# Layer 0 of a hybrid attention network: projections in two column tiles, column biases for both heads at once, and the first unit ahead of the branch

## The chip, the cores and the metric

The kernel runs on one core of a Trainium2 chip. The metric is the device time of one execution in microseconds (us). All arithmetic is in float32. A core has these engines: PE (TensorE: weight loads and matrix products), DVE (VectorE), ACT (ScalarE), POOL (GpSimd), and SP, which here only starts transfers. Each engine works through its own queue in order and waits for the others with semaphores.

## The reference, cut to what matters

The network has four layers on an image of 2 x 64 x 64 pixels with 128 channels. The change touches layer 0 alone, an attention with relative position biases, 4 heads of 32 dimensions and 4096 pixels for each of the 2 images:

```python
qkv = jnp.einsum('bhwc,cd->bhwd', x, w_qkv)          # x is the group-normalised input
...
pos = relative_position_bias(pos_q, pos_emb_h, pos_emb_w).reshape(B, nh, L, L)
scores = jnp.einsum('bnqd,bnkd->bnqk', q, k) * scale + pos
attn = jax.nn.softmax(scores, axis=-1)
out = jnp.einsum('bnqk,bnkd->bnqd', attn, v)
```

The bias of a query pixel (x, y) and a key pixel (x', y') is a row part, q times a row embedding that depends on x' - x, plus a column part, q times a column embedding that depends on y' - y. The result is added to the input. Three more layers follow: a triangle product, an attention without softmax with a mixture of experts behind it, and a softmax attention with a second mixture.

## The kernel before, in words

`layer0` first transposes the input to channels by pixels (`xT`) and normalises it, image by image. For each image it also takes the largest squared length of a pixel's vector (`l0sq`, the products `l0n`, the maximum `l0most`). From these and the weights it bounds the scores. The program then branches (L384): if the bound is small enough, which it is for this input, `l0_bounded` runs, where softmax needs no maximum; otherwise `l0_any` runs.

`l0_bounded` works through 8 units: image b, pair of heads, and half of the queries (2048 of them). A unit has 4 query groups of 512 (`qb`), and each group goes over 32 blocks of 128 keys. One block is:

- 4 products on PE for the scores of two heads, `l0sc` (L590). The operand `ka` holds for each head 32 rows of keys and 32 rows that are a one-hot code of the key's row; the operand `qa` holds 32 rows of queries and 32 rows of row bias. So the row part of the bias comes out of the same product.
- on ACT the exponential of the 128 x 1024 scores into `l0es` (L598).
- on DVE the product of this with `ew`, the exponential of the column part of the bias (L601).
- 4 products on PE with the values, `l0o` (L549), issued two blocks later.

Two buffers hold scores, three hold `l0es`, and two PSUM buffers, called `misc`, serve everything else. What the next unit needs is made meanwhile by a generator, `l0_prepare`. After every second block the loop takes one piece of it, up to its next yield (`piece`). A second list of odd work (`extra`: statistics for layer 1, and the head of layer 1 for the first image) is taken up after every fourth block. The listed order is then rearranged by the framework's scheduler, engine by engine; data dependencies stay.

`l0_prepare` of a unit consists of
- `l0pq`: 4 products that project the queries, with weights `wqk`, a copy of the weights spread so that the two heads of a pair land on rows 0 to 31 and 64 to 95. Each result is copied by ACT and by DVE into the two planes of `qa`.
- `l0pw`: the column bias, 64 columns y times 2 heads, each a product with a weight window of its own from the embedding table `pe` and 32 columns of queries; 8 exponentials on ACT write `ew`; two transfers copy the results to the other 64 partitions.
- `l0ph`: the row bias, 64 products, 16 copies into `qa`.
- for the first half of a pair, `l0pk`: 8 products that project the keys, 16 copies into `ka`.

The first unit has nothing to be hidden behind, and its whole `l0_prepare` runs after the branch. The values of an image (`l0_values`, 32 products, 8 copies) are made before its first `l0o`.

Of the kernel before, what the change touches and what calls it, by code (L numbers as in the profile page):

```python
# [14 lines left out]
P = 128  # L15
# [24 lines left out]
class Net:  # L40
# [216 lines left out]
    def layer0(self, xT, gst, na, nb):  # L257
# [3 lines left out]
        with ExitStack() as st:  # L261
# [3 lines left out]

            pe = wp.tile([P, 2, 2 * S - 1], F32, tag="pe", name="l0pe")
            with (
# [5 lines left out]
                for i, n in enumerate("hw"):  # L273
                    nc.scalar.dma_start(
                        out=raw[: 2 * S - 1, i, :], in_=ins[f"L0_conv_pos_emb_{n}"]
                    )
                    pt = ps.tile([P, 512], F32, tag="misc", name=f"l0pe{n}")
                    nc.tensor.transpose(pt[:HD, :P], raw[:, i, :], self.ident)
                    for lo in (0, 64):
                        nc.scalar.copy(pe[lo : lo + HD, i, :], pt[:HD, : 2 * S - 1])  # L280
# [68 lines left out]
                most = ap.tile([P, 4], F32, tag="most", name="l0most")  # L349
                for b in range(B):  # L350
# [3 lines left out]
                    for half in range(2):  # L354
                        part = xT[:, b, half * 2048 : (half + 1) * 2048]
                        nc.vector.tensor_scalar(part, part, gm, gr, ALU.subtract, ALU.mult)
                        sq = ap.tile([P, 2048], F32, tag="sq", name=f"l0sq{b}_{half}")
                        if half:
                            nc.gpsimd.tensor_tensor(sq, part, part, ALU.mult)
                        else:  # L360
                            nc.scalar.activation(sq, part, AF.Square)
                        pn = ps.tile([P, 512], F32, tag="misc", name=f"l0n{b}_{half}")
                        for i in range(4):
                            nc.tensor.matmul(
                                pn[HD * i : HD * (i + 1), :],
                                lhsT=ones,
                                rhs=sq[:, i * 512 : (i + 1) * 512],
                                start=True,
                                stop=True,
                            )  # L370
                        nc.vector.tensor_reduce(
                            most[:, 2 * b + half : 2 * b + half + 1], pn, AX.X, ALU.max
                        )
# [10 lines left out]
                small = self.at_most("l0", s1, 60.0)  # L384
            with tc.If(small > 0) as fits:
                self.l0_bounded(xT, w, pe, gst, na, nb)
            with fits.Else():
                self.l0_any(xT, w, pe)
# [78 lines left out]
    def l0_bounded(self, xT, w, pe, gst, na, nb):  # L467
# [15 lines left out]
        with (  # L483
# [4 lines left out]

            wqk = wp.tile([P, 2, 2, 2, 64], F32, tag="wqk", name="wqk")
            nc.vector.memset(wqk, 0.0)  # L490
            nc.vector.tensor_copy(
                wqk[:, :, :, :, :HD].rearrange("p j a h d -> p (j a h) d"),
                w[:, : 2 * C].rearrange("p (g d) -> p g d", d=HD),
            )
            kas = []
            for i in range(2):
                ka = wp.tile([P, L], F32, tag=f"ka{i}", name=f"ka{i}")
                for lo in (32, 96):
                    for half in range(2):
                        nc.gpsimd.tensor_copy(  # L500
                            ka[lo : lo + 32, half * H2 : (half + 1) * H2].rearrange(
                                "p (x y) -> p x y", y=S
                            ),
                            self.ident[lo : lo + 32, lo : lo + 32]
                            .unsqueeze(2)
                            .broadcast_to([32, 32, S]),
                        )
                kas.append(ka)
            v1 = wp.tile([P, NC, NH, HD + 1], F32, tag="v1", name="l0v1")
            nc.vector.memset(v1[:, :, :, HD:], 1.0)  # L510
# [8 lines left out]
            made = {}  # L519
            side, extra = [], []  # L520

# [15 lines left out]
            side.append(self.l0_prepare(ap, ps, units[0], xT, wqk, pe, kas, made))  # L537
            ready(units[0])
            waiting = []

            def values():
                unit, qb, k, es = waiting.pop(0)
                b, pair, half = unit
                if k == 0 and (pair, half, qb) == (0, 0, 0):
# [11 lines left out]
                if k == NC - 1:  # L556
# [5 lines left out]
                    if (b, pair, half, qb) == (0, 1, 1, 3):  # L562

                        extra.append(
                            self.l1_first(ps, xT[:, 0, :], gst[:, 0], w[:, : 2 * C], na, nb)
                        )
# [7 lines left out]
            for i, unit in enumerate(units):  # L574
# [4 lines left out]
                if i + 1 < len(units):  # L579
                    side.append(self.l0_prepare(ap, ps, units[i + 1], xT, wqk, pe, kas, made))  # L580
# [33 lines left out]
    def l0_prepare(self, ap, ps, unit, xT, wqk, pe, kas, made):  # L614
# [7 lines left out]
        qa = ap.tile([P, 2, H2], F32, tag="qa", name=f"l0qa{t}")  # L622
        ew = ap.tile([P, 2, H2], F32, tag="ew", name=f"l0ew{t}")
        for g in range(H2 // 512):
            cols = slice(g * 512, (g + 1) * 512)
            pq = ps.tile([P, 512], F32, tag="misc", name=f"l0pq{t}_{g}")
            nc.tensor.matmul(
                pq,
                lhsT=wqk[:, 0, pair, :, :].rearrange("p h d -> p (h d)"),
                rhs=xT[:, b, half * H2 + g * 512 : half * H2 + (g + 1) * 512],  # L630
                start=True,
                stop=True,
            )
            nc.scalar.copy(qa[:, 0, cols], pq)
            nc.vector.tensor_copy(qa[:, 1, cols], pq)
            yield
        for g in range(4):

            pw = ps.tile([P, 16, S // 2], F32, tag="misc", name=f"l0pw{t}_{g}")
            for i in range(16):  # L640
                y = 16 * g + i
                for lo in (0, 64):
                    nc.tensor.matmul(  # L643
                        pw[lo : lo + 64, i, :],
                        lhsT=pe[lo : lo + HD, 1, S - 1 - y : 2 * S - 1 - y],
                        rhs=qa[lo : lo + HD, 0, y::S],
# [3 lines left out]
                if i % 8 == 7:  # L650
                    yield
            for h in range(2):
                rows = slice(64 * h, 64 * h + 64)
                dst = ew[rows, h, :].rearrange("p (x y) -> p y x", y=S)
                nc.scalar.activation(dst[:, 16 * g : 16 * g + 16, :], pw[rows], AF.Exp)

        nc.sync.dma_start(out=ew[64:128, 0, :], in_=ew[0:64, 0, :])
        nc.sync.dma_start(out=ew[0:64, 1, :], in_=ew[64:128, 1, :])
# [22 lines left out]
        if half == 0:  # L681
            ka = kas[pair]
            root = float(HD) ** -0.5
            for g in range(L // 512):
                cols = slice(g * 512, (g + 1) * 512)
                pk = ps.tile([P, 512], F32, tag="misc", name=f"l0pk{b}_{pair}_{g}")
                nc.tensor.matmul(
                    pk,
                    lhsT=wqk[:, 1, pair, :, :].rearrange("p h d -> p (h d)"),
                    rhs=xT[:, b, cols],  # L690
                    start=True,
                    stop=True,
                )
# [1560 lines left out]
```

## Time and profile before

| what | value |
|---|---|
| time, median of 3 runs | 4827.95 us (4826.84 to 4828.98) |
| profiled execution, its own time | 4826.12 us |
| its span, first to last instruction | 4824.3 us |
| PE busy | 4514.4 us |
| DVE busy | 2918.7 us |
| ACT busy | 2661.0 us |
| POOL busy | 945.1 us |
| branch taken | about 58.2 us |
| first `l0o` of the first unit | 115.48 us |
| last `l0o` of layer 0 | about 2130 us |

Busy time is the time in which an engine has an instruction under way. Every float32 product appears in the profile as two records; a transpose appears as one. A number such as 64*33 after the names of a matmul is the part of the array that it uses, contraction rows by output rows. "[0.73 <-ACT l0os L558]" means that the engine stood idle for 0.73 us before the instruction and that the named instruction ended this. Layer 0 fills the first 2131 us of the span.

### The profile page before, as it was taken

What the parts mean: (1) busy time and instruction counts of PE and PEld (TensorE: products, weight loads), DVE (VectorE), ACT (ScalarE), POOL (GpSimd) and SP (SyncE); (2) the same over time, 40 slices, a digit from 0 to 9 for tenths busy, and PEclk for the clock granted to TensorE, in tenths of its full rate; (3) what the DMA queues carried; (4) which work ended last, traced back from release to release, by engine and by line L of the source; (5) the groups of instructions that cost most, each with busy time, mean ns of one, the idle gap of its engine ahead of it and who ended that gap; (6) DMA issues with size and microseconds to landing.
All of it is one profiled execution on the core that took longest, in us unless ns stands there. A gap on an engine that the chain in (4) does not pass through costs nothing.

```text
span 4824.3 us, 78221 instructions
## 1 busy us (share of the span) xinstructions
PE 4514.4 (94%) x33260; PEld 1761.8 (37%) x33260; DVE 2918.7 (61%) x4784; ACT 2661.0 (55%) x3091; POOL 945.1 (20%) x848
## 2 busy tenths in 40 slices
PE   6999999999999999978799999999977999999999
PEld 3333333333233333325322223322225444444443
DVE  4676767676766767766746666555553444454447
ACT  4666565655656565555667666676731444433326
POOL 1000000000000000004455454555531000000008
PEclk7999999999999999989899999999987999999999
DMA  1000000000000000000000000000025000000001
GB/s 46 10 1 10 1 10 1 10 1 10 1 1 10 1 12 1 1 6 21 6 1 1 1 1 1 1 1 1 1 93 194 1 1 0 1 0 1 0 1 36
DMA packets 43211, 60.30 MB, mean 12 GB/s; under 512 B 4352, under 2 KB 25056, under 8 KB 41696
## 3 DMA queue, kind: packets, MB, share of 16 engines
q1 hardware_dynamic: 41552, 54.34, 3.6%
q8 instruction: 265, 4.34, 0.4%
q10 hardware_dynamic: 1296, 0.82, 0.1%
q14 instruction: 98, 0.80, 0.1%
HBM read 42.56 MB, written 4.19 MB: 10 GB/s over the span
## 4 chain that ended last, share of the span: by engine, by line
PE 78%; DVE 9%; ACT 6%; POOL 3%; issue 2%; DMA 1%; SPq 0%; DVEq 0%; ACTq 0%; POOLq 0%
PE l0sc L590 17%; PE l0o L549 16%; PE scl L2076 9%; PE oTl L2035 9%; PE l2sc L1448 5%; PE l2pos L1195 5%; PE l2av L1494 3%; DVE l2es L1468 2%; PE f3ex L2185 2%; POOL l2es L1471 2%; PE l0pw L643 1%; ACT l2es L1479 1%; ACT l0es L598 1%; PE l1p L938 1%; ACT l2es L1459 1%
## 5 line engine op out<-in xcount | busy, mean ns | idle before, releaser
L601 DVE TENSOR_TENSOR l0es<-l0es,l0ew 128x1024 f32<-128x1024 f32 x1024 | 1253.4, 1228 | 586.4 <-ACT l0es L598 586.1
L598 ACT ACTIVATE l0es<-l0sc 128x1024 f32<-128x1024 f32 x1024 | 1042.8, 1024 | 676.2 <-PE l0sc L590 671.0
L549 PE MATMUL l0o<-l0es,l0v 64*33 64x512 f32 x8192 | 1068.0, 591 | 19.8 <-ACT l0os L558 12.5
L590 PE MATMUL l0sc<-l0qa,ka 64*64 64x512 f32 x8192 | 1080.6, 596 | 4.7 <-ACT l0es L598 4.7
L1479 ACT ACTIVATE l2es<-l2es 128x1024 f32<-128x1024 f32 (+3 forms) x576 | 559.5, 984 | 265.8 <-POOL l2es L1471 258.7
L1471 POOL TENSOR_TENSOR l2es<-l2es 128x1024 f32<-128x1024 f32 (+3 forms) x352 | 581.2, 1662 | 493.9 <-DVE l2es L1468 442.7
L2043 DVE TENSOR_TENSOR accl<-accl,esl 128x1024 f32<-128x1024 f32 x240 | 302.5, 1261 | 424.6 <-ACT esl L2087 421.2
L1468 DVE TENSOR_SCALAR l2es<-l2sc 128x1024 f32<-128x1024 f32 (+3 forms) x320 | 338.7, 1058 | 314.5 <-PE l2sc L1448 314.3
L2087 ACT ACTIVATE esl<-scl 128x1024 f32<-128x1024 f32 x240 | 245.6, 1023 | 485.2 <-PE scl L2076 460.1
L590 PEld LDWEIGHTS l0sc<-l0qa,ka 64*64 64x64 f32 x8192 | 294.3, 133 | 545.6 <-issue 478.4
L2076 PE MATMUL scl<-l3qT,l3kT 128*128 128x512 f32 x1024 | 487.4, 596 | 0.0
L549 PEld LDWEIGHTS l0o<-l0es,l0v 64*33 64x33 f32 x8192 | 257.2, 108 | 626.8 <-issue 559.2
L1448 PE MATMUL l2sc<-l2q,kept 32*128 32x512 f32 (+3 forms) x2304 | 391.3, 622 | 83.4 <-ACT l2es L1459 58.9
L2035 PE MATMUL oTl<-esl,l3v 128*128 128x512 f32 x960 | 451.1, 592 | 0.0
L724 POOL TENSOR_TENSOR x<-x,l0y 128x256 f32<-128x256 f32 x32 | 23.4, 731 | 2037.1 <-DVE l0y L719 1912.6
L1494 PE MATMUL l2av<-l2es,kept 128*32 128x512 f32 (+3 forms) x2304 | 312.2, 592 | 0.0
L1195 PE MATMUL l2pos<-kept 128*32 128x512 f32 x2416 | 296.8, 599 | 0.1
L2035 PEld LDWEIGHTS oTl<-esl,l3v 128*128 128x128 f32 x960 | 181.7, 190 | 225.6 <-issue 222.0
L2076 PEld LDWEIGHTS scl<-l3qT,l3kT 128*128 128x128 f32 x1024 | 188.2, 191 | 207.5 <-issue 191.3
L1459 ACT ACTIVATE l2es<-l2sc 128x1024 f32<-128x1024 f32 x224 | 226.1, 1010 | 53.2 <-PE l2sc L1448 51.8
L1448 PEld LDWEIGHTS l2sc<-l2q,kept 32*128 32x128 f32 x2304 | 116.1, 187 | 328.3 <-ACT l2es L1459 160.2
L1195 PEld LDWEIGHTS l2pos<-kept 128*32 128x32 f32 x2416 | 78.4, 111 | 175.1 <-issue 174.3
(702 smaller groups left out, 3750.0 us busy)
## 6 DMA issues: line engine op xcount, KB each, us to landing
f2w<-in_L_ffn_weight_dram SPq DMA_DIRECT2D x32, 1024.0 KB, 13.1
l0ew<-l0ew SPq DMA_DIRECT2D x16, 512.0 KB, 5.0
x<-in_x_dram SPq DMA_DIRECT2D x8, 512.0 KB, 8.9
out_dram<-x SPq DMA_DIRECT2D x16, 256.0 KB, 2.3
kept<-in_L_attn_pos_rev_dram SPq DMA_DIRECT2D x1, 1792.0 KB, 6.7
ew<-in_L_ffn_expert_w_dram SPq DMA_DIRECT2D x1, 512.0 KB, 4.0
kept<-in_L_attn_pos_rev_dram SPq DMA_DIRECT2D x1, 256.0 KB
f2b<-in_L_ffn_weight_dram ACTq DMA_DIRECT2D x2, 128.0 KB, 2.7
```

What stands on the lines that cost most here:

```text
L549: nc.tensor.matmul(o[64 * h : 64 * h + HD + 1, r, :], lhsT=v1[rows, k, 2 * pair + h, :], rhs=es[rows, h, :], start=(k == 0), stop=(k == NC ...
L590: nc.tensor.matmul(sc[64 * c : 64 * c + 64, h, :], lhsT=ka[rows, k0 : k0 + 64], rhs=qa[rows, k // (NC // 2), qs], start=True, stop=True,)
L598: nc.scalar.activation(es, sc, AF.Exp)
L601: nc.vector.tensor_tensor(es, es, ew[:, :, qs], ALU.mult)
L1195: nc.tensor.matmul(out[part], lhsT=lhsT[:, part], rhs=rhs, start=start, stop=stop)
L1448: nc.tensor.matmul(sc[:, h2, off:], lhsT=kT[hs, k * P : (k + 1) * P], rhs=q[hs, off:], start=True, stop=True,)
L1468: nc.vector.tensor_scalar(es[:, :, lo:], sc[:, :, lo:], root, None, ALU.mult)
L1471: nc.gpsimd.tensor_tensor(part, part, part, ALU.mult)
L1479: nc.scalar.activation(es[:, :, off:], es[:, :, off:], AF.Silu)
L1494: nc.tensor.matmul(avs[i][hs, off:], lhsT=v[:, k, hs], rhs=es[h // 2][:, h % 2, off:], start=(k == 0), stop=last,)
L2035: nc.tensor.matmul(oT, lhsT=vs[b][:, k, :], rhs=es[:, i, :], start=(k == 0), stop=(k == NC - 1),)
L2076: nc.tensor.matmul(sc[:, i, :], lhsT=kTs[b][:, k * P : (k + 1) * P], rhs=qT[:, qb * 512 : (qb + 1) * 512], start=True, stop=True,)
```

## The change

In words:

- **Projections.** `wqk` is gone. A new helper, `projected`, issues two products of 64 output rows each (both heads of the pair, straight from `w`) for two neighbouring groups of 512 pixels, into the two halves of one PSUM tile. `l0pq` is thus called 2 times for a unit and not 4, `l0pk` 4 times for a pair and not 8.
- **Copies of the queries.** For every 512 queries there are now six copies out of PSUM, three on ACT (64 x 512, 32 x 256, 32 x 1024) and three on DVE (32 x 512, 32 x 256, 32 x 256), where there was one 128 x 512 on each. They place the queries of both heads side by side on rows 32 to 63 (columns y below 32) and 96 to 127 (the others). These rows hold the row bias later.
- **Column bias.** One product of a weight window now takes 64 columns, the queries of both heads: 64 products for a unit and not 128. The two row groups write two PSUM tiles at once, 8 of them to a piece. The exponentials stay 8 of 64 x 512. One transfer of 1024 KB replaces two of 512 KB.
- **First unit.** Its `l0_prepare`, its one-hot rows and the values of the first image are issued ahead of the branch, mixed with the maxima. For this the two images are transposed and normalised first, and the maxima follow. `qa` and `ew` are now tiles outside the branch (`qe`, and `qe1` for every second unit).
- `l1_first` gets a tile of its own (`gb`) for what it wrote over the projection weights before, since `w` is still read. `l0_any` is adapted and isn't run for this input.

```diff
+            qe = wp.tile([P, 2, 2, L // 2], F32, tag="qe", name="l0qe")
+            ka = wp.tile([P, L], F32, tag="ka", name="ka0")
+            self.l0_hot(ka, 0)
+            self.l0_hot(ka, 1)
+            v = wp.tile([P, NC, NH, HD + 1], F32, tag="v1", name="l0v1")
...
-                    for lo in (0, 64):
-                        nc.scalar.copy(pe[lo : lo + HD, i, :], pt[:HD, : 2 * S - 1])
+                    for lo in range(0, P, 32):
+                        copy = nc.vector.tensor_copy if lo % 64 else nc.scalar.copy
+                        copy(pe[lo : lo + HD, i, :], pt[:HD, : 2 * S - 1])
...
+                first = self.l0_prepare(
+                    ps, (0, 0, 0), xT, w, pe, [ka], (qe[:, 0], qe[:, 1]), made
+                )
...
+                for b in range(B):
+                    for half in range(2):
+                        pieces(4)
+                        lengths(b, half)
...
                 small = self.at_most("l0", s1, 60.0)
+                for _ in first:
+                    pass
+                self.l0_values(ps, 0, xT, w, v)
             with tc.If(small > 0) as fits:
-                self.l0_bounded(xT, w, pe, gst, na, nb)
+                self.l0_bounded(xT, w, pe, gst, na, nb, qe, ka, v)
...
+        def projected(j, g, name):
+
+            out = ps.tile([P, 512], F32, tag="misc", name=name)
+            for i in range(2):
+                nc.tensor.matmul(
+                    out[64 * i : 64 * i + 64, :],
+                    lhsT=w[:, j * C + 64 * pair : j * C + 64 * pair + 64],
+                    rhs=xT[:, b, (g + i) * 512 : (g + i + 1) * 512],
+                    start=True,
+                    stop=True,
+                )
+            return out
+
+        for g in range(0, H2 // 512, 2):
+            pq = projected(0, half * (H2 // 512) + g, f"l0pq{t}_{g}")
+            for i in range(2):
+                cols = slice((g + i) * 512, (g + i + 1) * 512)
+                p0 = pq[64 * i : 64 * i + 32]
+                p1 = pq[64 * i + 32 : 64 * i + 64]
+                left = [
+                    v.rearrange("p (x y) -> p x y", y=S)[:, :, : S // 2]
+                    for v in (qa[32:64, 0, cols], p0)
+                ]
+                yield
+                nc.scalar.copy(qa[:64, 1, cols], pq[64 * i : 64 * i + 64])
+                nc.vector.tensor_copy(qa[:HD, 0, cols], p0)
+                yield
+                nc.vector.tensor_copy(left[0], left[1])
+                for h, p in ((0, p0), (1, p1)):
+                    right = [
+                        v.rearrange("p (x y) -> p x y", y=S)[:, :, S // 2 :]
+                        for v in (qa[96:128, h, cols], p)
+                    ]
+                    (nc.scalar.copy if h else nc.vector.tensor_copy)(right[0], right[1])
+                nc.scalar.copy(
+                    qa[64 : 64 + HD, :, cols], p1.unsqueeze(1).broadcast_to([HD, 2, 512])
+                )
             yield
         for g in range(4):
-            pw = ps.tile([P, 16, S // 2], F32, tag="misc", name=f"l0pw{t}_{g}")
-            for i in range(16):
-                y = 16 * g + i
-                for lo in (0, 64):
+            pw = [
+                ps.tile([P, 8, 2, S // 2], F32, tag="misc", name=f"l0pw{t}_{g}_{i}")
+                for i in range(2)
+            ]
+            for n in range(8):
+                for i, lo in ((0, 32), (1, 96)):
+                    y = 32 * i + 8 * g + n
                     nc.tensor.matmul(
-                        pw[lo : lo + 64, i, :],
+                        pw[i][:S, n, :, :],
                         lhsT=pe[lo : lo + HD, 1, S - 1 - y : 2 * S - 1 - y],
-                        rhs=qa[lo : lo + HD, 0, y::S],
+                        rhs=qa[lo : lo + HD, :, y::S],
                         start=True,
                         stop=True,
                     )
...
-        nc.sync.dma_start(out=ew[64:128, 0, :], in_=ew[0:64, 0, :])
-        nc.sync.dma_start(out=ew[0:64, 1, :], in_=ew[64:128, 1, :])
+        nc.sync.dma_start(out=ew[S:], in_=ew[:S])
...
-            for g in range(L // 512):
-                cols = slice(g * 512, (g + 1) * 512)
-                pk = ps.tile([P, 512], F32, tag="misc", name=f"l0pk{b}_{pair}_{g}")
+            for g in range(0, L // 512, 2):
+                pk = projected(1, g, f"l0pk{b}_{pair}_{g}")
                 yield
-                nc.scalar.activation(ka[:HD, cols], pk[:HD], AF.Copy, scale=root)
-                nc.vector.tensor_scalar(
-                    ka[64 : 64 + HD, cols], pk[64 : 64 + HD], root, None, ALU.mult
-                )
+                for i in range(2):
+                    cols = slice((g + i) * 512, (g + i + 1) * 512)
+                    lo = 64 * i
+                    nc.scalar.activation(ka[:HD, cols], pk[lo : lo + HD], AF.Copy, scale=root)
+                    nc.vector.tensor_scalar(
+                        ka[64 : 64 + HD, cols], pk[lo + HD : lo + 64], root, None, ALU.mult
+                    )
```

In the order in which the engines of the changed kernel get their instructions, the copies of a pair of query groups stand close together. Around blocks 7 to 11 of a unit's first query group ACT's queue is: exponential 7, copy 64 x 512, exponential 8, copies 32 x 256, 32 x 1024 and 64 x 512, exponential 9, copies 32 x 256 and 32 x 1024, exponential 10. DVE's queue is: product 7, copies 32 x 512, 32 x 256, 32 x 256, product 8, the same three copies, product 9. The second of ACT's copies waits for DVE's third, the first of DVE's waits for ACT's first, and so on along one PSUM tile.

## The prediction

> **What bounds the kernel now.** I read the page first, for the bound and the chain that ended last.
>
> ```profile
> span 4824.3 us, 78221 instructions
> ...
> PE 4514.4 (94%) x33260; PEld 1761.8 (37%) x33260; DVE 2918.7 (61%) x4784; ACT 2661.0 (55%) x3091; POOL 945.1 (20%) x848
> ...
> PE 78%; DVE 9%; ACT 6%; POOL 3%; issue 2%; DMA 1%; SPq 0%; DVEq 0%; ACTq 0%; POOLq 0%
> PE l0sc L590 17%; PE l0o L549 16%; PE scl L2076 9%; PE oTl L2035 9%; PE l2sc L1448 5%; PE l2pos L1195 5%; PE l2av L1494 3%; DVE l2es L1468 2%; PE f3ex L2185 2%; POOL l2es L1471 2%; PE l0pw L643 1%; ACT l2es L1479 1%; ACT l0es L598 1%; PE l1p L938 1%; ACT l2es L1459 1%
> ```
>
> PE sets the time, and layer 0's loop is a third of the chain. Next, busy time by stretches (width, then PE, PEld, DVE, ACT, POOL, granted clock):
>
> ```profile
> 58.00:102.00 44.00, 34.88 (x412) 22.61 (x414) 15.17 (x23) 19.55 (x27) 14.96 (x8) 0.64 0.11 25
> 102.00:340.00 238.00, 236.35 (x2370) 86.87 (x2370) 159.19 (x144) 145.43 (x154) 2.19 (x3) 1.00 0.03 6
> 1181.27:1197.15 15.88, 13.95 (x92) 5.54 (x88) 8.04 (x18) 6.90 (x8) 0.00 (x0) 0.68 0.00 1
> ```
>
> In the loop PE is full (236 of 238 us); ACT and DVE are not (145, 159). So whatever leaves PE's queue there shortens the layer. The start, 58 to 102, is no PE bound: the first unit is made alone, at a clock of 0.64. Third, PE in order of time, where a piece's price can be read:
>
> ```profile
> 121.87 1.04 PE L549 MATMUL l0o<-l0es,l0v 64*33 64x512 f32 x8
> 122.84 1.12 PE L627 MATMUL l0pq<-xT,wqk 128*128 128x512 f32 x2
> ...
> 126.52 1.04 PE L549 MATMUL l0o<-l0es,l0v 64*33 64x512 f32 x8
> ...
> 131.17 1.04 PE L549 MATMUL l0o<-l0es,l0v 64*33 64x512 f32 x8
> 132.14 1.13 PE L643 MATMUL l0pw<-l0qa,l0pe 32*64 32x32 f32 x32
> ...
> 168.37 1.04 PE L549 MATMUL l0o<-l0es,l0v 64*33 64x512 f32 x8
> 169.34 1.15 PE L666 MATMUL l0ph<-l0qa,l0pe 32*64 32x64 f32 x32
> ...
> 173.04 1.04 PE L549 MATMUL l0o<-l0es,l0v 64*33 64x512 f32 x8
> ```
>
> Two blocks without a piece take 3.44 us (`l0o` at 207.93 and 211.37). With a `l0pq` piece they take 126.52 - 121.87 = 4.65, with `l0pw` (131.17 to 135.82) 4.65, with `l0ph` 4.67. A piece costs 1.21, 1.21 and 1.24 us; `l0pk` (454.50 to 459.15) 1.21.
>
> **Pieces removed, units 2 to 8.** `l0pq`: 4 to 2 pieces, 7 x 2 x 1.21 = 16.9 us. `l0pk`: 8 to 4, in 3 units, 3 x 4 x 1.21 = 14.5. `l0pw`: 8 pieces of 16 products to 4 of 16 with twice the columns, 7 x (8 x 1.21 - 4 x 1.24) = 33.0. Together **64.4 us**.
>
> Two prices aren't in the trace. Two 128 x 64 products side by side cost 1.21 if they overlap, 2.07 if not (one more 0.86, `l0pq`'s pace). I take 1.21: the four 128*32 tiles of `l0n` ran as 8 records in 1.94 us at a cold clock, where 8 x 0.43 = 3.44 at full clock would be one after another. The new `l0pw` piece is 32 records of 64 columns, two row groups over the same array columns. Near row: `l0ph`, same size, 1.24. Low end 1.21; high end 2.06 if nothing overlaps (32 x 0.43 x 64/512 = 1.71, and 0.35 for switching, which is what a `l0pq` piece costs above its 2 x 0.43). I take 1.24, since `l0sc` overlaps row groups over the same columns.
>
> **What ACT and DVE pay.** Before, 512 queries cost ACT 0.585 and DVE 0.69. Now ACT has 64 x 512 (0.58), 32 x 256 (between 0.29 and 0.575; 0.36 by the line through 32 x 512 at 0.575 and 97 x 1024 at 1.009) and 32 x 1024 (1.01); DVE has 0.69 and two of 32 x 256 (0.35 to 0.69; 0.42, as L719 with 128 x 256). By busy time that is hidden: per unit 4 x 1.4 us more on ACT, in 250 us with 90 idle. But it comes in a burst, and the two engines take turns on one PSUM tile, as today:
>
> ```profile
> 170.59 0.57 ACT L677 COPY l0qa<-l0ph 32x512 f32<-32x512 f32 x1 [0.62 <-PE l0ph L666]
> 171.48 0.68 DVE L677 COPY l0qa<-l0ph 32x512 f32<-32x512 f32 x1
> 172.20 0.58 ACT L677 COPY l0qa<-l0ph 32x512 f32<-32x512 f32 x1 [1.03 <-DVE l0qa L677]
> 172.80 1.94 ACT L598 ACTIVATE l0es<-l0sc 128x1024 f32<-128x1024 f32 x2
> 172.81 0.70 DVE L677 COPY l0qa<-l0ph 32x512 f32<-32x512 f32 x1 [0.64 <-ACT l0qa L677]
> ```
>
> ACT stands 1.03 us for DVE, with the next exponential queued behind it. PE doesn't notice, because every second block brings another piece, 1.24 us of cover. In the changed order the copies of one `l0pq` tile fall into four blocks without a piece. I follow the three queues, with `l0sc` 8 starting at 0, an `l0sc` or `l0o` each 0.86, an exponential 1.02 and a product with `ew` 1.23:
> - ACT: copy to 0.74, exponential 8 to 2.22, wait for DVE's third copy (to 2.37), three copies 2.41 to 4.43, exponential 9 to 5.48, wait for DVE's sixth (to 6.05), two copies to 7.49, exponential 10 to 8.54.
> - DVE: three copies 0.78 to 2.37, product 8 to 3.63, wait for ACT's fourth copy, three copies 4.47 to 6.05, product 9 to 7.31, product 10 to 9.81.
> - PE, with two score buffers and `l0o` two blocks behind: `l0sc` 11 is due at 5.21 and waits for exponential 9 (0.34); `l0o` 9 for product 9 (0.96); `l0sc` 12 for exponential 10 (0.37); `l0o` 10 for product 10 (0.41). After that the queues catch up.
>
> That is 2.1 us a tile; 14 tiles in units 2 to 8: **29.4 us given back**.
>
> A pair of `l0pw` exponentials holds ACT for 2.14 us. The exponential behind it ends 3.33 us after its `l0sc` began, its product with `ew` at 4.6, and `l0o` is due at 4.30. Today the next piece covers that; the new `l0pw` pieces stand four blocks apart. 28 x 0.35 = **9.8 us**. The key copies keep a piece every second block, as `l0ph` today: nothing.
>
> [...] The idle shares alone would give 0 for this step, 39 us less; [...]
>
> **The first unit.** Before, the branch is at 58.15 and the first `l0o` at 115.48, with `l0sc` 0 to 2, one `l0pq` and the values done. After, in the order of the changed queues:
> - Both images' statistics come first. Image 0's ends at 27.7. DVE then has 8 statistics of image 1 (0.61 each), image 0's chain and its two scalings (2.6), to 36.7; image 1's chain 3.45 and scalings, to 42.8. PE's first `l0pq` stands behind image 1's chain, at about 39.
> - Two tiles of turns, 7.2 us each for six copies on either engine, and four maxima on DVE (0.69), to about 55.
> - On ACT a table load (1.28) and six exponentials (1.05), to 63; the bound's root with two more loads, to 66; two exponentials, 68.5.
> - `l0ph`'s 8 copies on ACT with their waits 5.5, keys 5, values 8 x 0.59: 84.5. ACT is the longest queue; PE and DVE wait for it.
> - Branch 0.9 (58.1 to 59.0 today), `l0sc` 0 at 85.4, `l0o` 0 four us later (product and exponential between), at 89.5.
>
> Gain **26 us**; 18 to 34, as the turns overlap less or more.
>
> Beside it: POOL's one-hot copies (4 x 1.9 us) move to the start, where POOL is idle until 31.8; `ka1`'s follow the branch, two units before use. Behind SP's transfer stands only its branch load. 1024 KB: 10 us as two of 5.0, 13.1 as the weights' row; issued at 68.5, wanted at 87. Later units have some 90 blocks. If it came late, product 0 would wait for it. The memsets of `l0o` and `l0os` (2 x 0.91 on DVE) run during the first scores. The four copies into `pe` on DVE (about 0.26, ACT's row at 9.29) fit in DVE's idle 1.42 us before 16.58.
>
> **Sum.** 4826.1 (the profiled execution) - 26 - 64.4 + 39.2 = 4774.9. The median of the runs is 1.8 above the profiled one: **4776 us**.
>
> **Rivals.**
> - *The bursts cost nothing*: 4776 - 39 = 4737. For: today's bursts cost nothing. Against: the cover is gone.
> - *Tiles don't overlap*: the `l0pw` piece at 2.06 gives 28 x 0.82 = 23 back, 4799; the column pairs at 2.07, 26 x 0.86 = 22, 4798. The second would be a change that doesn't do what it says. `l0n` and `l0sc` speak against both.
> - *The start gains nothing*: ACT's serial queue ends as late as today's, 4802. With the tiles too: about 4825, no change.
> - *Slower: each burst drops the clock.* It happens today, once:
>
> ```profile
> 1184.59 0.35 PE L135 MATMUL gpv<-gv,gmat 128*128 128x1 f32 x2 [1.93 <-DVE gv L133]
> ...
> 1188.55 1.91 PE L643 MATMUL l0pw<-l0qa,l0pe 32*64 32x32 f32 x30
> ```
>
> After that wait a piece took 1.91, and the stretch (clock 0.68) 15.9 us where 3 blocks (5.2), a piece (1.2) and the statistics' products (1.5) make 7.9: 8 lost. At 8 x 14 = 112: 4888. It decides from 3.7 us a burst. [...] and `l0o` at 189.99 resumed at full pace after 0.73. I go by these.
>
> **How the numbers follow.** Forecast 0.48; bursts free 0.17; tiles 0.18; start 0.09; start and tiles 0.03; clock 0.05. Range: 4734 takes in the free bursts, 4804 the tiles and the start; outside lie the clock and double cases. 0.2% (9.7 us) is about what the measurement tells from no change. Faster 0.92, same 0.03, slower 0.05.
>
> **What would show it.** `l0pq`, `l0pk` and `l0pw` pieces at 1.2 us between `l0o`; PE waits of 0.3 to 1 us for `l0es` on ACT and DVE after each `l0pq`; first `l0o` near 90. Wrong if a `l0pw` piece takes 2 us, PE never waits after `l0pq`, the clock falls below 1 in the loop, or the first `l0o` is past 105.

## The result, and the profile after

The changed kernel takes 4785.74 us (median of 4 runs, 4780.16 to 4790.27), against 4827.76 for the kernel before on the same chip: a ratio of 0.9912 (95% interval 0.9895 to 0.9929), 42 us or 0.9% faster. The forecast was 4776. The sum holds a large error that a smaller one of the other sign half hides, so the agreement says less than it seems to. The profiled execution took 4783.74, its span is 4781.9, so 42.4 us less than before. The page of the changed kernel:

```profile
span 4781.9 us, 76270 instructions
...
PE 4464.8 (93%) x32236; PEld 1739.6 (36%) x32236; DVE 2943.9 (62%) x4850; ACT 2697.7 (56%) x3157; POOL 945.6 (20%) x848
...
PE 75%; DVE 11%; ACT 7%; issue 3%; POOL 2%; DMA 1%; SPq 0%; DVEq 0%; ACTq 0%; POOLq 0%
```

PE is still the bound, with 50 us less work. The chain that ended last now runs over DVE for 11% and ACT for 7%, where it was 9 and 6, and PE spends some of what it no longer does waiting. PE in order of time (start, duration, engine, line, operation, what is written and read, part of the array, shape, count, and idle time before with what ended it), first the start of the loop and one `l0pq` piece:

```profile
87.41 1.95 PE L615 MATMUL l0sc<-l0qe,ka 64*64 64x512 f32 x16
...
91.68 1.06 PE L573 MATMUL l0o<-l0es,l0v 64*33 64x512 f32 x8 [0.29 <-DVE l0es L626]
...
596.83 1.04 PE L573 MATMUL l0o<-l0es,l0v 64*33 64x512 f32 x8
597.80 1.08 PE L657 MATMUL l0pq<-xT,wqkv 128*64 128x512 f32 x4
...
599.72 1.04 PE L573 MATMUL l0o<-l0es,l0v 64*33 64x512 f32 x8
...
603.15 1.04 PE L573 MATMUL l0o<-l0es,l0v 64*33 64x512 f32 x8
604.24 1.09 PE L615 MATMUL l0sc<-l0qe,ka 64*64 64x512 f32 x8
606.08 1.06 PE L573 MATMUL l0o<-l0es,l0v 64*33 64x512 f32 x8 [0.74 <-DVE l0es L626]
607.30 1.09 PE L615 MATMUL l0sc<-l0qe,ka 64*64 64x512 f32 x8 [0.16 <-ACT l0es L623]
608.55 1.06 PE L573 MATMUL l0o<-l0es,l0v 64*33 64x512 f32 x8 [0.17 <-DVE l0es L626]
...
610.30 1.04 PE L573 MATMUL l0o<-l0es,l0v 64*33 64x512 f32 x8
```

The first `l0o` comes at 91.68 (115.48 before). The `l0pq` piece with its two column tiles costs 599.72 - 596.83 - 1.72 = 1.17 us, no more than the single product before, so the tiles overlap. Then come four late starts: `l0sc` at 604.24, `l0o` at 606.08, `l0sc` at 607.30 and `l0o` at 608.55 are 0.23, 0.98, 0.36 and 0.39 us later than the pace of 0.86 allows. From 596.83 to 610.30 it takes 13.47 us, where six blocks (10.30) and the piece make 11.47: the tile costs PE 2.0 us more. Of the 13 `l0pq` tiles in the loop, 11 cost between 1.95 and 2.03 us in this way; behind the other two another product follows at once. ScalarE's queue in the same time:

```profile
601.14 0.36 ACT L686 COPY l0qe<-l0pq 32x256 f32<-32x256 f32 x1 [0.15 <-DVE l0qe L686]
601.53 1.00 ACT L687 COPY l0qe<-l0pq 32x1024 f32<-32x1024 f32 x1
602.56 0.58 ACT L677 COPY l0qe<-l0pq 64x512 f32<-64x512 f32 x1
603.17 1.02 ACT L623 ACTIVATE l0es<-l0sc 128x1024 f32<-128x1024 f32 x1
604.80 0.37 ACT L686 COPY l0qe<-l0pq 32x256 f32<-32x256 f32 x1 [0.61 <-DVE l0qe L686]
605.19 1.01 ACT L687 COPY l0qe<-l0pq 32x1024 f32<-32x1024 f32 x1
606.22 1.94 ACT L623 ACTIVATE l0es<-l0sc 128x1024 f32<-128x1024 f32 x2
```

Three copies stand ahead of one exponential and two ahead of the next. The `l0pw` piece of the changed kernel:

```profile
637.50 1.04 PE L573 MATMUL l0o<-l0es,l0v 64*33 64x512 f32 x8
638.47 1.98 PE L701 MATMUL l0pw<-l0qe,l0pe 32*64 32x64 f32 x32
640.38 1.09 PE L615 MATMUL l0sc<-l0qe,ka 64*64 64x512 f32 x8
641.28 1.04 PE L573 MATMUL l0o<-l0es,l0v 64*33 64x512 f32 x8
```

The `l0pw` piece costs 641.28 - 637.50 - 1.72 = 2.06 us. So one of the prediction's own signs of being wrong came true: "Wrong if a `l0pw` piece takes 2 us".

For the whole loop I added up the time between the starts of neighbouring `l0sc` and `l0o` beyond their pace (0.858 us for each group of 8 records), by what lies between. In us, number in brackets:

| between | before | after |
|---|---|---|
| `l0pq` | 31.5 (27) | 14.6 (13) |
| `l0pk` | 28.0 (24) | 13.4 (12) |
| `l0pw` | 64.2 (55) | 57.4 (28) |
| `l0ph` | 33.8 (28) | 33.3 (28) |
| nothing but waits for `l0es` (DVE, ACT or unnamed at `l0sc`) | 15.1 | 39.5 |
| first to last `l0o` | 2013.9 | 1995.8 |

The head gave 23.8 us and the loop 18.1, together the 41.9 by which the last `l0o` comes earlier (2129.35 to 2087.47). The rows make 14.4 of the loop's 18.1 us; the rest is spread over small waits. The `l0pw` row understates the saving: one old piece stands beside statistics and isn't in it, and each piece delays the pair behind it by some 0.05 us more. Taken from `l0o` to `l0o`, as in the prediction, an old `l0pw` piece costs 1.22 us, a new one 2.06 and an `l0ph` piece 1.24.

### The profile page after: what moved, and what is told of

It is laid out like the page before. It is cut to its first block, busy times and chain, and to the rows that moved or that the text cites. A ratio compares the mean times of both kernels' runs of the same rounds, so it can differ in the third digit from the quotient of the medians.

```text
span 4781.9 us, 76270 instructions
## 1 busy us (share of the span) xinstructions
PE 4464.8 (93%) x32236; PEld 1739.6 (36%) x32236; DVE 2943.9 (62%) x4850; ACT 2697.7 (56%) x3157; POOL 945.6 (20%) x848
## 4 chain that ended last, share of the span: by engine, by line
PE 75%; DVE 11%; ACT 7%; issue 3%; POOL 2%; DMA 1%; SPq 0%; DVEq 0%; ACTq 0%; POOLq 0%
PE l0o L573 15%; PE l0sc L615 15%; PE scl L2126 9%; PE oTl L2085 9%; PE l2sc L1498 5%; PE l2pos L1245 5%; PE l2av L1544 3%; PE f3ex L2235 2%; DVE l2es L1518 2%; POOL l2es L1521 2%; ACT l0es L623 2%; ACT l2es L1529 1%; DVE l0es L626 1%; PE l0pw L701 1%; PE l1p L988 1%
## 5 line engine op out<-in xcount | busy, mean ns | idle before, releaser
L626 DVE TENSOR_TENSOR l0es<-l0es,l0qe 128x1024 f32<-128x1024 f32 x1024 | 1250.2, 1228 | 529.5 <-ACT l0es L623 528.4
L615 PE MATMUL l0sc<-l0qe,ka 64*64 64x512 f32 x8192 | 1080.3, 595 | 5.7 <-ACT l0es L623 5.0
L2137 ACT ACTIVATE esl<-scl 128x1024 f32<-128x1024 f32 x240 | 245.8, 1024 | 485.0 <-PE scl L2126 451.7
L615 PEld LDWEIGHTS l0sc<-l0qe,ka 64*64 64x64 f32 x8192 | 298.5, 133 | 568.0 <-issue 490.4
L1509 ACT ACTIVATE l2es<-l2sc 128x1024 f32<-128x1024 f32 x224 | 226.3, 1010 | 52.5 <-PE l2sc L1498 51.3
```

The costliest lines, as they stand in the source:

```text
L615: nc.tensor.matmul(sc[64 * c : 64 * c + 64, h, :], lhsT=ka[rows, k0 : k0 + 64], rhs=qa[rows, k // (NC // 2), qs], start=True, stop=True,)
L626: nc.vector.tensor_tensor(es, es, ew[:, :, qs], ALU.mult)
```

## The experiments

Two questions were open. Why does the new `l0pw` piece take 2.06 and not 1.24 us? And do the waits after `l0pq` come from the burst of copies? Runs of one comparison share a chip with the kernel before, which took 4827.1 to 4831.4 (medians) on the four chips used; so differences in us between rows of the table can be off by some 4 us. "Loop" is first to last `l0o` in the profile; it and the first `l0o` come from one execution each. No ratio is given where there was one run.

| run | us, median | ratio to before, 95% interval | first `l0o` | loop |
|---|---|---|---|---|
| the changed kernel | 4785.74 | 0.9895 to 0.9929 | 91.68 | 1995.8 |
| e1_columns | 4794.15 | 0.9910 to 0.9943 | 92.51 | 2002.2 |
| e2_contiguous | 4757.55 | 0.9836 to 0.9869 | 88.27 | 1971.9 |
| e3_copies_by_dma | 4751.31 | 0.9822 to 0.9854 | 86.83 | 1965.8 |
| e4_head_undone | 4804.41 | 0.9931 to 0.9964 | 105.23 | 1999.3 |
| e5_spread | 4783.56 | 0.9889 to 0.9922 | 86.87 | 1997.4 |
| e6_y_order | 4746.91 | 0.9813 to 0.9846 | 85.20 | 1963.2 |
| e7_pairs | 4755.24 | | 90.37 | 1972.0 |
| e8_step4 | 4783.91 | | 89.88 | 1996.9 |
| e9_y_order_pool | 4732.03 | 0.9783 to 0.9816 | 87.53 | 1944.5 |
| e10_y_order_split | 4736.43 | 0.9789 to 0.9822 | 86.32 | 1954.1 |
| e11_one_group_a_piece | 4769.87 | 0.9858 to 0.9891 | 89.47 | 1983.3 |

### The column-bias piece: array columns or reading order?

**e1_columns**

```diff
-                        pw[i][:S, n, :, :],
+                        pw[i][64 * i : 64 * i + S, n, :, :],
...
-                nc.scalar.activation(dst[:, y : y + 8], pw[i][:S], AF.Exp)
+                nc.scalar.activation(dst[:, y : y + 8], pw[i][64 * i : 64 * i + S], AF.Exp)
```

> The second row group of a column-bias piece writes array columns 64 to 127 (PSUM partitions 64 to 127 of its own bank) in place of the columns of the first; both banks, the strided queries and every other instruction stay. Theory 1, two row groups that end in the same columns do not run together: the l0pw piece falls from 2.06 to the 1.24 us of an l0ph piece, 28 x 0.82 = 23 us, about 4763 us. Theory 2, reading the queries at a stride of 64 elements sets the pace: 2.06 stays, about 4786. Theory 3, taking turns between two banks costs: 2.06 stays, about 4786.

**e2_contiguous**

```diff
-                        rhs=qa[lo : lo + HD, :, y::S],
+                        rhs=qa[lo : lo + HD, :, S * (8 * g + n) + 32 * i : S * (8 * g + n) + 32 * i + 32],
```

> The column-bias products read 32 neighbouring queries of each head in place of 32 at a stride of 64 elements; the column biases are therefore those of other queries, and the output is not the reference's. Array columns and banks stay as in the changed kernel. Theory 1 (same columns) and theory 3 (two banks): the l0pw piece stays at 2.06 us, about 4786 us. Theory 2 (the stride): it falls to about 1.24, about 4763.

The groups of `l0pw` by shape (line, result and inputs, array, shape, count, busy us, mean ns of a record, idle before), first of the changed kernel with `l0ph` for comparison, then of e1_columns, then of e2_contiguous:

```profile
L701 PE MATMUL l0pw<-l0qe,l0pe 32*64 32x64 f32 x1024 | 65.9, 284 | 8.2 <-DVE l0qe L680 8.2
L723 PE MATMUL l0ph<-l0qe,l0pe 32*64 32x64 f32 x1024 | 39.2, 231 | 0.0
```

```profile
L701 PE MATMUL l0pw<-l0qe,l0pe 32*64 32x64 f32 x1024 | 66.0, 285 | 8.5 <-DVE l0qe L680 8.5
```

```profile
L701 PE MATMUL l0pw<-l0qe,l0pe 32*64 32x64 f32 x1024 | 43.8, 229 | 2.2 <-ACT l0qe L712 2.2
```

Other columns leave the piece as it was (2.05): theory 1 falls. Neighbouring queries, with the same columns and the same two banks, bring the record to that of `l0ph` and the piece to 1.21; the loop is 23.9 us shorter, as the piece's 28 x 0.84 = 23.5. So theory 2 stands, and theories 1 and 3 fall with this run. The 8 us by which e1_columns is slower aren't in its pieces: its loop is 6.4 us longer, and on the count of the table above its waits for `l0es` make 45.5 us and not 39.5. Why was not tested.

**e7_pairs and e8_step4** ask what about the reading order costs: the step of 256 bytes, or that each element is read alone, with no neighbour beside it. Their times are of one run each; what counts is the piece.

```diff
-                        rhs=qa[lo : lo + HD, :, y::S],
+                        rhs=qa[lo : lo + HD].rearrange("p h (r c) -> p h r c", c=S)[
+                            :, :, 16 * (n % 2) : 16 * (n % 2) + 16, 32 * i + 8 * g + n // 2 * 2 : 32 * i + 8 * g + n // 2 * 2 + 2
+                        ],
```

> The column-bias products read, of each head, 16 pairs of neighbouring queries, one pair every 64 elements; the column biases are those of other queries and the output is not the reference's. [...] if it is the step of 256 bytes itself (or any reading out of order), it stays near 2.05, or halfway (1.6) if each step costs once.

e8_step4 has `:, :, 4 * n : 4 * n + 4, 32 * i + g : 32 * i + 32 : 4` there instead.

> The column-bias products read, of each head, 4 rows of 8 queries at a step of 4 elements (16 bytes); the column biases are those of other queries and the output is not the reference's. [...] if it is that of the long step of 256 bytes, it falls to about 1.2.

The same group, of e7_pairs and of e8_step4:

```profile
L701 PE MATMUL l0pw<-l0qe,l0pe 32*64 32x64 f32 x1024 | 43.4, 228 | 4.0 <-DVE l0qe L680 3.2 <-DVE l0most L385 0.4 <-ACT l0qe L686 0.3
```

```profile
L701 PE MATMUL l0pw<-l0qe,l0pe 32*64 32x64 f32 x1024 | 70.1, 287 | 2.3 <-DVE l0qe L680 1.3 <-ACT l0qe L714 0.7
```

Pairs at a step of 256 bytes cost nothing that shows (piece 1.21); single elements at a step of only 16 bytes cost all (2.08). So in these products it is not the length of the step: single elements cost at both steps, pairs at the longer one don't. The price of single elements is 284 to 287 ns a record against 228, and 0.84 us for a piece of 64 columns a product. Steps between 4 and 16 bytes were not tried.

Why had the old piece not paid? Its group in the kernel before:

```profile
L643 PE MATMUL l0pw<-l0qa,l0pe 32*64 32x32 f32 x2048 | 75.0, 230 | 1.0 <-ACT l0qa L634 0.7 <-ACT l0ew L655 0.3
```

Its products read 32 single elements. At the new piece's pace, 2.05 us for 32 records of 64 columns, a column costs about 1.0 ns and 32 columns 32 ns, an estimate. A record of these small products came every 37 ns all the same (1.17 us / 32), and no faster with 64 neighbours (1.21 / 32 = 38). By this estimate the penalty was there before but lay below this floor, and twice the columns put it on top; no run varies the columns alone. The same floor limits what e7_pairs shows: its 64 elements come as 32 pairs, and if a pair costs what a single element does, 1.0 ns, they would again take 32 ns; so the runs can't tell whether the elements of a pair are read at the pace of neighbours or cost together as much as one alone.

### The waits after `l0pq`: the burst of copies?

**e3_copies_by_dma**

```diff
                 yield
                 nc.scalar.copy(qa[:64, 1, cols], pq[64 * i : 64 * i + 64])
...
+            yield
+            cols = slice(g * 512, (g + 2) * 512)
+            for lo, kh, h in ((0, 0, 0), (32, 0, 0), (64, 0, 1), (64, 1, 1), (96, 0, 0), (96, 1, 1)):
+                nc.sync.dma_start(
+                    out=qa[lo : lo + 32, kh, cols], in_=qa[32 * h : 32 * h + 32, 1, cols]
+                )
+            yield
...
```

The other five copies are gone, and four empty pieces stand ahead of the column biases.

> Of the six copies that follow each 512 projected queries one stays, ScalarE's 64x512 (0.58 us); the other places of the queries are filled by six SBUF-to-SBUF DMAs per 1024 queries, with four empty pieces before the column biases. If the burst of copies is what delays l0es: the waits of l0sc and l0o on l0es after each l0pq tile go, 14 x 2.0 = 28 us, about 4758 us (up to 3 us of it lost at the start, where the first column biases wait for the DMAs). Rival, the waits come from the l0pq product itself taking the place of a score block: they stay, about 4786. Rival, the DMAs land after the first column-bias product is reached and TensorE stands behind it: waits of l0pw on a DMA appear, 4786 to 4800.

4751.3, 34 us below the changed kernel: in the profiled executions 4.9 from an earlier first `l0o`, against the loss that I had allowed for, and 30.0 from the loop. Of these 30.0, waits for `l0es` make 21 (18.1 are left); the rest is spread over small waits and the statistics. PE after an `l0pq` piece of e3_copies_by_dma:

```profile
600.55 1.08 PE L657 MATMUL l0pq<-xT,wqkv 128*64 128x512 f32 x4
...
604.18 1.04 PE L573 MATMUL l0o<-l0es,l0v 64*33 64x512 f32 x8
605.04 1.04 PE L615 MATMUL l0sc<-l0qe,ka 64*64 64x512 f32 x8
605.90 1.04 PE L573 MATMUL l0o<-l0es,l0v 64*33 64x512 f32 x8
...
611.05 1.04 PE L573 MATMUL l0o<-l0es,l0v 64*33 64x512 f32 x8
```

Block after block at 1.72 us, with no wait, behind all 13 tiles of the loop; both rivals fall (no `l0pw` product waited for a DMA). But the copies are gone altogether here, so this doesn't yet tell their bunching from their amount.

**e5_spread** was to separate bunching from the amount of copying:

```diff
                 nc.scalar.copy(qa[:64, 1, cols], pq[64 * i : 64 * i + 64])
+                yield
                 nc.vector.tensor_copy(qa[:HD, 0, cols], p0)
                 yield
                 nc.vector.tensor_copy(left[0], left[1])
+                yield
                 for h, p in ((0, p0), (1, p1)):
...
+                yield
                 nc.scalar.copy(
```

> The same six copies per 512 projected queries, on the same engines, but in five pieces in place of two, so that at most one copy of each engine falls between two score blocks. If the waits after l0pq come from bunching (two or three copies of an engine ahead of one exponential), they go: about 28 us off, 4758 us. If they come from the amount of copying (2.0 us of ScalarE and 1.5 of VectorE for each 512 queries), or from any copy longer than the room in a piece, most of them stay: 4775 to 4786.

4783.6, no change, but it isn't the test that I meant: the scheduler put the copies back together. ACT of e5_spread around one tile:

```profile
595.84 0.36 ACT L688 COPY l0qe<-l0pq 32x256 f32<-32x256 f32 x1 [0.16 <-DVE l0qe L688]
596.22 1.00 ACT L690 COPY l0qe<-l0pq 32x1024 f32<-32x1024 f32 x1
597.25 0.58 ACT L677 COPY l0qe<-l0pq 64x512 f32<-64x512 f32 x1
597.85 1.02 ACT L623 ACTIVATE l0es<-l0sc 128x1024 f32<-128x1024 f32 x1
599.49 0.36 ACT L688 COPY l0qe<-l0pq 32x256 f32<-32x256 f32 x1 [0.61 <-DVE l0qe L688]
599.88 1.00 ACT L690 COPY l0qe<-l0pq 32x1024 f32<-32x1024 f32 x1
```

Two sets stand on either side of one exponential, as in the changed kernel. Here the yields moved instructions in the program's order, not in the queue.

**e11_one_group_a_piece** spaces the sets by something that the scheduler can't move, the product that they wait for:

```diff
-        for g in range(0, H2 // 512, 2):
-            pq = projected(0, half * (H2 // 512) + g, f"l0pq{t}_{g}")
-            for i in range(2):
+        for g in range(H2 // 512):
+            pq = ps.tile([P, 512], F32, tag="misc", name=f"l0pq{t}_{g}")
+            nc.tensor.matmul(
+                pq[:64, :],
+                lhsT=w[:, 64 * pair : 64 * pair + 64],
+                rhs=xT[:, b, half * H2 + g * 512 : half * H2 + (g + 1) * 512],
+                start=True,
+                stop=True,
+            )
+            for i in range(1):
```

> l0pq takes 512 queries a piece again (one product into half a PSUM tile, 4 pieces a unit), with the changed kernel's six copies for each; in the queues one set of copies then stands alone, with five to six exponentials between two sets, where the changed kernel has two sets on two exponentials. The 14 more pieces cost 14 x 1.2 = 17 us. If two sets close together cause the stalls, they go (28 us) and the sum is 4785.7 + 17 - 28 = 4775 us. If each set stalls TensorE by itself (1.0 us a set or more), it is 4785.7 + 17 = 4803 us, less what a shorter piece saves in stalls.

4769.9: 16 us faster than the changed kernel, with 14 pieces more. The pieces cost 30.0 - 14.6 = 15.4 us, and the waits for `l0es` fall from 39.5 to 16.5, about as low as before the change (15.1); behind none of its 27 `l0pq` pieces in the loop is there one. A set of this run on ACT, and PE meanwhile:

```profile
593.10 0.58 ACT L684 COPY l0qe<-l0pq 64x512 f32<-64x512 f32 x1 [0.78 <-PE l0pq L668]
594.14 1.02 ACT L623 ACTIVATE l0es<-l0sc 128x1024 f32<-128x1024 f32 x1 [0.47 <-PE l0sc L615]
595.31 0.36 ACT L693 COPY l0qe<-l0pq 32x256 f32<-32x256 f32 x1
595.70 1.00 ACT L694 COPY l0qe<-l0pq 32x1024 f32<-32x1024 f32 x1
596.73 1.94 ACT L623 ACTIVATE l0es<-l0sc 128x1024 f32<-128x1024 f32 x2
```

```profile
595.61 1.04 PE L573 MATMUL l0o<-l0es,l0v 64*33 64x512 f32 x8
596.47 1.04 PE L615 MATMUL l0sc<-l0qe,ka 64*64 64x512 f32 x8
597.33 1.04 PE L573 MATMUL l0o<-l0es,l0v 64*33 64x512 f32 x8
598.19 1.04 PE L615 MATMUL l0sc<-l0qe,ka 64*64 64x512 f32 x8
```

The same copies, one set at a time: the exponential behind them is late by less than the two score buffers and the lag of `l0o` give, and ACT catches up with two exponentials in a row. Nor do the added pieces hide the copies: the next one comes only after six blocks, at 603.49, and these six run at 1.72 us each. So it is two sets close together that PE pays for. Pairing the query projections gained 16.9 us of PE and cost some 23, the waits that go here.

### The first unit

**e4_head_undone**

```diff
-                first = self.l0_prepare(
-                    ps, (0, 0, 0), xT, w, pe, [ka], (qe[:, 0], qe[:, 1]), made
-                )
...
-                for _ in first:
-                    pass
-                self.l0_values(ps, 0, xT, w, v)
...
-            made = {units[0]: places[0]}
+            made = {}
...
+            side.append(self.l0_prepare(ps, units[0], xT, w, pe, kas, places[0], made))
+            ready(units[0])
```

> The first unit is prepared after the branch again, with the changed kernel's own pieces; nothing else is put back. Theory, the earlier start is worth what the first l0o moved, 23.8 us: the first l0o comes at about 115 us, the last one about 24 us later than in the changed kernel, about 4809 us. Rival, part of the 23.8 comes from work that the change dropped (the padded weights, the constants ahead of the loop): the first l0o comes at 100 to 108 us, 4794 to 4802.

The first `l0o` is at 105.2, as the rival has it, but the loop is longer too (the first values, `l0pv`, now lie in it: 16.5 us against 7.6), so the last `l0o` comes 17.0 us later and the median is 18.7 above. Neither number was right. Of the 23.8 us by which the first `l0o` moved, some 17 to 19 belong to the move; the other 5 to 7 remain with this head as well, and which dropped work they are is open. The bounds are rough: kernels with the changed kernel's head and pieces as slow as its own have their first `l0o` anywhere from 89.88 (e8_step4) to 92.51 (e1_columns).

### Both causes taken away

**e6_y_order**, **e9_y_order_pool** and **e10_y_order_split** compute the right biases with neighbouring queries. They keep ScalarE's 64x512 copy and three of the DMAs of e3_copies_by_dma, and write the queries in y order:

```diff
+                    own = qa[32 * h : 32 * h + 32, 1, cols].rearrange("p (x y) -> p x y", y=S)
+                    for half_y, copy in ((0, nc.vector.tensor_copy), (1, nc.scalar.copy)):
+                        lo = 32 + 64 * half_y
+                        to = qa[lo : lo + 32, 0, :].rearrange("p (h y x) -> p h x y", h=2, x=S // 2)
+                        copy(
+                            to[:, h, n0 // S : n0 // S + 8, :],
+                            own[:, :, 32 * half_y : 32 * half_y + 32],
+                        )
...
-                        rhs=qa[lo : lo + HD, :, y::S],
+                        rhs=qa[lo : lo + HD, 0, :].rearrange(
+                            "p (h y x) -> p h y x", h=2, x=S // 2
+                        )[:, :, 8 * g + n, :],
```

e9_y_order_pool has `nc.gpsimd.tensor_copy` for both copies (and four empty pieces more ahead of the column biases), e10_y_order_split VectorE and GpSimd.

> The queries of the column biases are laid down by column (y) first, so that the 32 queries of one column lie next to each other; the duplicates of whole rows go by DMA as in the run before. Per 512 queries: one ScalarE copy of 64x512 from PSUM, and four of 32x256 from SBUF to SBUF, two on each engine, in pieces of their own. Right biases. If stride and bursts are what costs, both gains add: 4785.7 - 34 (copies by DMA) - 28 (neighbouring queries) = 4723, and up to 10 us back if the new copies delay exponentials: 4720 to 4735. If the two gains overlap (both open the same waits), no better than 4745.

4746.9 misses the forecast of 4720 to 4735. It is near the number for gains that overlap (4745), but they don't, as the next run shows: the `l0pw` piece is at 1.19, and a burst is back, this time from SBUF to SBUF, at 1.3 us for 12 of the 13 tiles. ACT of e6_y_order, and PE:

```profile
579.98 1.19 ACT L672 COPY l0qe<-l0pq 64x512 f32<-64x512 f32 x2 [0.80 <-PE l0pq L657]
581.19 1.91 ACT L679 COPY l0qe<-l0qe 32x256 f32<-32x256 f32 x3
583.13 1.02 ACT L623 ACTIVATE l0es<-l0sc 128x1024 f32<-128x1024 f32 x1
```

```profile
584.20 1.09 PE L615 MATMUL l0sc<-l0qe,ka 64*64 64x512 f32 x8 [0.67 <-ACT l0es L623]
585.46 1.06 PE L573 MATMUL l0o<-l0es,l0v 64*33 64x512 f32 x8 [0.17 <-DVE l0es L626]
```

Five copies stood ahead of one exponential. ACT took no turns with DVE on a PSUM tile here, and PE waits all the same (0.67 and 0.17 us): a full queue of ACT is enough here.

> As e6_y_order (right biases), but GpSimd makes the four copies of 32x256 that put the queries in y order, so that ScalarE keeps one copy of 0.58 us per 512 queries and VectorE none. If the stalls that e6_y_order kept (about 1.9 us for each of 14 l0pq tiles) come from three ScalarE copies of 0.64 us bunched between two exponentials, they go: 4746.9 - 27 = 4720 us. If GpSimd's copies are slow (over 1.5 us each), l0pw products stand for them, in the loop or in the first unit: 4725 to 4745.

> As e6_y_order (right biases), but VectorE makes two and GpSimd two of the four y-order copies. If only ScalarE's bunch costs, this equals e9_y_order_pool; if VectorE's bunch (four copies of 0.39 us between two products) costs too, some 0.6 us a tile, it is 8 us above it.

With GpSimd the stalls behind `l0pq` are gone at all 13 tiles: 4732.0, the fastest kernel here, 2.0% below the kernel before and 54 us below the changed one. The loop is 51.3 us shorter than the changed kernel's, near the sum of the two causes taken alone (23.9 + 30.0). It missed 4720: the first `l0o` is at 87.53 (85.20 in e6_y_order), and some 18 us of waits of `l0o` for VectorE remain, most of them at statistics and output pieces. GpSimd's copies took 1.1 us each, and no `l0pw` in the loop waited for them. e10_y_order_split is 4.4 us above it in the median, where 8 were forecast, but its loop is 9.6 us longer; the rest of the program, the same in both, ran 4 us shorter in the profiled execution. So VectorE's bunch seems to cost too; how much is not settled.

## Why the prediction was right, and where not

- **First unit**: 23.8 us at the first `l0o`, against 26. `l0sc` 0 came at 87.41, 85.4 forecast. The copies of `ka1` ran at 67, ahead of the first scores; nothing waited for them. The large transfer landed in 6.7 us.
- **Column pairs**: 1.17 for `l0pq` against 1.21, and savings of 16.9 and 14.6, against 16.9 and 14.5. The tiles overlap.
- **The step that failed** is the price of the new `l0pw` piece: "I take 1.24, since `l0sc` overlaps row groups over the same columns". It took 2.06, so the pieces save 7 x (8 x 1.21 - 4 x 2.06) = 10.1 us and not 33.0. That the upper end of 2.06 fits is luck: it was worked out for products that don't overlap, while over the same columns `l0sc` does overlap (8 records of 512 columns in 0.86 us, the time of two at 0.43) and so, by e2_contiguous, do these (the piece at 1.21, where the prediction's estimate for one record after another is 1.71); what is slow is reading the queries as single elements (284 ns a record against 229). The near row was badly chosen. `l0ph` has the same number of columns but reads neighbours; the old `l0pw` has the same reading order but half the columns, and its equal price (230 ns a record to 231), by the estimate above, hid the penalty.
- **Bursts**: 2.0 us at the tile shown, against 2.1, as four delays of 0.23, 0.98, 0.36 and 0.39 where the three queues had given 0.34, 0.96, 0.37 and 0.41. Over the loop it is 22 us at 11 of its 13 tiles, against 29.4 at 14; two meet another piece, and some 4 us of waits follow the tile just ahead of the first `l0o`. All waits for `l0es` grew by 24.4 us.
- **Exponential pairs**: the 9.8 us aren't there. Apart from stretches with statistics, waits of `l0sc` after `l0pw` add up to some 4 us, to under 1 in e2_contiguous, where the piece is as short as I had assumed, so a longer piece is not what hides them. What does is open.
- **Clock**: 0.99 to 1.00 in the long stretches of the loop (102 to 1181 and 1197 to 2087 us), bursts included. That rival was out. The other sign named, a clock below 1 in the loop, did come in one place, but behind statistics of layer 1 and not behind a burst:

```profile
1174.08 1.93 PE L573 MATMUL l0o<-l0es,l0v 64*33 64x512 f32 x8 [3.63 <-DVE l1mv L169]
```

After this wait the clock was 0.60 until 1181, and 0.52 from 1187 to 1190, after one of 2.26 us. The kernel before fell there too (0.68, 1181 to 1197), behind a wait of only 1.93; and in e8_step4 the two `l0sc` after the same wait of 3.63 kept the pace of a full clock, 0.86 and 0.89 us behind the `l0o` ahead of each. So the length of a single wait, by which the prediction judged, doesn't settle it here. Behind the bursts PE stood idle for at most 0.74 us at a time at the tile shown.

In sum: 22.9 us lost at the piece, 2.2 at the start, 14.8 won back at the waits: 10 us, where the median is off by 10. Without the 9.8 us for the exponential pairs, for which nothing came, the forecast would have been off by some 20 us: the nearness is in part luck.

## What to carry to other kernels

When a product is widened, look at how its moving operand is read: single elements cost nothing that showed here at 32 columns a product (230 ns a record) and made the piece 70% longer at 64 (2.05 us, against 1.21 with neighbours), so a row with the same shape but another reading order is no near row. When PE work is merged into fewer pieces, the copies that hang on it come merged too; what an engine has in its queue ahead of one critical instruction decided here (39.5 us of waits for `l0es` with two sets of copies together, 16.5 with one at a time), not its idle share. Space such copies by what they depend on (4769.9 us here, against 4785.7), or give them to an idle queue (4751.3 with DMA; GpSimd took the stalls away at all 13 tiles), since a scheduler that is free to reorder can undo an order given only in the program, as in e5_spread.

## What the runs showed of the hardware that I had not expected

- In products of 64 columns, pairs of float32 at a step of 256 bytes take no longer than 32 neighbours of each head (228 and 229 ns a record); single ones at a step of 16 bytes are as slow as at 256 (287 and 284).
- A 32x256 copy into y order took ScalarE 0.63 us (0.36 for the plain copy out of PSUM), VectorE 0.43 (0.42). Source and order differ both, so the order alone is not shown to be the cause.
- VectorE's 32x256 copy rose from 0.43 to 0.66 us on average when GpSimd did its half of the same work beside it. GpSimd's own took 0.75, or 1.1 when it had all four. Why was not tested.
